# Two-layer interaction network: difference of x made on GpSimd from its own buffers, first stage of layer 2 in pieces, a third buffer for sums of products

## Chip, cores, metric

One core of a Trainium2 chip. The metric is the device time of one execution in microseconds (us). "Span" is the time from the first to the last instruction of the profiled execution, some 1.7 us less. Engines: PE is TensorE (PEld its weight loads), DVE VectorE, ACT ScalarE, POOL GpSimd, SP SyncE, which only issues loads here.

## The reference, cut

```python
# x: 4096 rows, 32 fields, 16 values; all float32
def _cin_layer(out, x, W, b, gamma, beta):
    h = jnp.einsum('rne,rfe->rnfe', out, x).reshape(r, -1, e)    # all products of fields
    h = jnp.einsum('rce,oc->roe', h, W) + b[None, :, None]       # 128 outputs
    return _batchnorm(h, gamma, beta)                            # mean and variance over rows and values
h1 = _cin_layer(x, x, W1, ...)                  # layer 1: 32 x 32 products
out, direct1 = (h1[:, :64], h1[:, 64:])
direct2 = _cin_layer(out, x, W2, ...)           # layer 2: 64 x 32 products
return concatenate([direct1, direct2], axis=1).sum(axis=-1)
```

## The kernel before

The columns (row, value) are cut into 128 tiles of 512. Layer 1 takes one tile after another: two loads of 0.5 MB, one product z on VectorE, five matmuls, three ScalarE copies out of PSUM (the memory that TensorE writes its sums to, in banks). Layer 2 goes in 64 chunks of two tiles, with Strassen's scheme: per chunk four stages, each with two factors f (ScalarE, into PSUM), two products z1 and z2 (VectorE, 128x2048), three sums t of these (GpSimd, not in the first stage) and 14 or 16 matmuls into four PSUM banks. Then `combine` puts the banks together, spread over the stages of the next chunk. z2 needs, beside x, differences of x. These are made in layer 1, one for every 16 chunks, and stored to DRAM:

```python
rpool = one.enter_context(tc.tile_pool(name="rpool", bufs=2))
...
def difference(g):
    xs = []
    for j in (2, 0):
        x = rpool.tile([P, 2 * T], FP, tag="r", name="x")          # the buffers of load_rem
        ...
        nc.sync.dma_start(x, bass.AP(xb.tensor, at, [...]))
        xs.append(x)
    nc.vector.tensor_tensor(xs[0], xs[0], xs[1], ALU.subtract)     # VectorE
    nc.scalar.dma_start(diffs[g], xs[0])                           # issued by ScalarE
...
    with tc.issue_after(loads[-1].ins):                            # loop over the tiles t of layer 1
        if t % 16 == 12 and t // 16 < NC // DIFF:
            difference(t // 16)
...
psum = ctx.enter_context(tc.tile_pool(name="psum", bufs=6, ...))   # banks; a chunk of layer 2 takes 4
tpool = ctx.enter_context(tc.tile_pool(name="tpool", bufs=2))      # sums of products
...
def combine(c, sums_):
    x62, x34, x57, x11 = sums_.banks
    act(both[low], x11[high])                                      # ScalarE
    act(both[high], x11[low], bias=b2[low])
    yield
    add(both, both, x11)                                           # VectorE
    yield
    add(e[:, 0], both, x62)
    yield
    ...
for c in range(NC):                                                # layer 2
    f1 = factor(raw[STAGES[0]], STAGES[0], 0)
    for k, i in enumerate(STAGES):
        z1 = multiply(f1, b, "z")
        if k in (1, 2, 3):
            step()                                                 # one step of the chunk before
        f2 = factor(raw[i], i, 1)
        ...
        z2 = multiply(f2, bx, "z2")
        ...
        if k < 3:
            f1 = factor(raw[STAGES[k + 1]], STAGES[k + 1], 0)
        if k == 0:
            step(2)                                                # both copied, both added
        ...
```

A scheduler places the instructions of each engine in an order of its own; `issue_after` adds an edge only to an instruction on the same engine.

## Time and profile before

2178.69 us, median of 3 runs (2177.85 to 2179.77). Three points of the timeline cut the span: "keep" is the small VectorE copy that ends the statistics of layer 1; "last t of chunk 0" is the matmul that waits for the last sum of products in the first chunk of layer 2; then the end.

| before | us |
|---|---|
| keep starts | 533.1 |
| from keep to the matmul on the last t of chunk 0 | 33.9 |
| from there to the end | 1608.2 |
| span | 2175.2 |

The page's lines by slice (40 equal slices, tenths busy) show TensorE near full nearly throughout, and a granted clock (PEclk) of 9 tenths or more in all but the last slice, where TensorE has run out of work. The dips, stretches of 3.4 or 6.8 us at half clock, are too short to show in such coarse slices. The prediction shows finer windows.

```profile
PE   7998899999999999999999999999999999999995
...
PEclk9999999999999999999999999999999999999998
```

### The profile page before, as it was taken

How to read it: one execution, taken by the hardware profiler on the slowest of the kernel's cores; microseconds unless marked ns; L12 is line 12 of the kernel's file. 1: busy time of each engine (PE TensorE's matmuls, PEld its weight loads, DVE VectorE, ACT ScalarE, POOL GpSimd, SP SyncE). 2: the span in 40 equal slices, each digit the busy share in tenths (PEclk: the TensorE clock that was granted, in tenths of full speed). 3: DMA queues.
4: the chain of work that ended last, by engine and by line, in shares of the span. 5: the costliest groups of instructions: out<-in, count | busy, mean ns of one | idle time of the engine just before them, and what ended most of it. 6: DMA issues, size and time to landing. Idle time of an engine off the chain costs nothing.

```text
span 2175.2 us, 23541 instructions
## 1 busy us (share of the span) xinstructions
PE 2104.6 (97%) x8716; PEld 736.2 (34%) x8716; DVE 1909.9 (88%) x1422; ACT 854.4 (39%) x1221; POOL 1355.8 (62%) x582
## 2 busy tenths in 40 slices
PE   7998899999999999999999999999999999999995
PEld 3333343443333333333333333333333333333331
DVE  7876888887899989999988999998999998999995
ACT  3444444454333333433333333333333333333332
POOL 0000000000888888888888788888788888788884
PEclk9999999999999999999999999999999999999998
DMA  9999999997766777666777666777766777766751
GB/s 344 321 313 316 321 353 332 347 354 239 174 165 165 173 171 173 161 165 165 171 171 173 163 164 161 171 172 171 168 163 160 171 171 174 169 157 163 171 129 39
DMA packets 111700, 440.65 MB, mean 203 GB/s; under 512 B 13024, under 2 KB 13024, under 8 KB 102880
## 3 DMA queue, kind: packets, MB, share of 16 engines
q1 hardware_dynamic: 104992, 416.33, 71.3%
q10 hardware_dynamic: 6592, 22.81, 2.9%
q8 instruction: 68, 1.11, 0.2%
q14 instruction: 48, 0.39, 0.1%
HBM read 417.07 MB, written 22.02 MB: 202 GB/s over the span
## 4 chain that ended last, share of the span: by engine, by line
PE 42%; POOL 27%; DVE 10%; issue 9%; DMA 8%; ACT 2%; SPq 1%; DVEq 0%; POOLq 0%; ACTq 0%
PE x L416 32%; POOL t L432 27%; PE ps L307 9%; DMA b<-in_xb 5%; DVE z L390 4%; DVE z L295 4%; ACT both L383 2%; DMA x<-in_xb 1%; DMA r<-in_xr 1%; DVE stats L97 1%; PE ps L305 1%; DMA a<-in_xa 0%; DVE e L386 0%; DMA h<-kept 0%; SPq L200 0%
## 5 line engine op out<-in xcount | busy, mean ns | idle before, releaser
L416 PE MATMUL x<-z,w_sb 128*64 128x512 f32 x2560 | 1076.3, 594 | 0.0
L416 PE MATMUL x<-z,s_sb 128*64 128x512 f32 x2048 | 954.7, 594 | 4.5 <-DVE z L390 4.5
L432 POOL TENSOR_TENSOR t<-z,z 128x1024 f32<-128x1024 f32 x192 | 456.8, 2379 | 779.7 <-DVE z L390 779.7
L432 POOL TENSOR_TENSOR t<-z,t 128x1024 f32<-128x1024 f32 x384 | 903.1, 2374 | 15.1
L416 PE MATMUL x<-t,s_sb 128*64 128x512 f32 x1536 | 698.4, 594 | 0.0
L383 ACT ACTIVATE f<-a,keep 128x512 f32<-128x512 f32 x512 | 398.3, 778 | 637.9 <-DVE z L390 635.1
L390 DVE TENSOR_TENSOR z<-f,b 128x2048 f32<-128x2048 f32 x256 | 582.5, 2275 | 0.9 <-ACT f L383 0.8
L390 DVE TENSOR_TENSOR z<-f,bx 128x2048 f32<-128x2048 f32 x256 | 582.7, 2276 | 0.0
L416 PEld LDWEIGHTS x<-z,w_sb 128*64 128x64 f32 x2560 | 334.7, 137 | 614.1 <-issue 613.8
L307 PE MATMUL ps<-z,w_sb 128*128 128x512 f32 x1024 | 461.5, 608 | 26.5 <-DVE z L295 26.1
L416 PE MATMUL x<-t,w_sb 128*64 128x512 f32 x768 | 363.4, 596 | 9.4 <-POOL t L432 9.4
L416 PEld LDWEIGHTS x<-z,s_sb 128*64 128x64 f32 x2048 | 281.4, 137 | 228.2 <-issue 222.0
L295 DVE TENSOR_TENSOR z<-a,b 128x2048 f32<-128x2048 f32 x128 | 291.8, 2282 | 46.2 <-DMA b<-in_xb 31.9
L307 PEld LDWEIGHTS ps<-z,w_sb 128*128 128x128 f32 x1024 | 195.0, 194 | 291.5 <-issue 234.3
L416 PE MATMUL x<-z,neg_sb 128*64 128x512 f32 x512 | 230.2, 592 | 0.0
L416 PEld LDWEIGHTS x<-t,s_sb 128*64 128x64 f32 x1536 | 205.3, 137 | 4.0 <-issue 4.0
L263 ACT ACTIVATE e<-ps,bn_sb 128x512 f32<-128x512 f32 x127 | 87.3, 687 | 276.2 <-PE ps L307 210.9
L416 PEld LDWEIGHTS x<-t,w_sb 128*64 128x64 f32 x768 | 100.1, 137 | 241.2 <-issue 172.1
L386 DVE TENSOR_TENSOR both<-both,x 128x512 f32<-128x512 f32 x64 | 44.0, 688 | 142.0 <-ACT both L383 142.0
L383 ACT ACTIVATE u<-e,bn_sb 64x512 f32<-64x512 f32 x64 | 46.2, 722 | 183.3 <-DVE e L386 183.3
L383 ACT ACTIVATE both<-x 64x512 f32<-64x512 f32 x64 | 38.0, 593 | 150.4 <-PE x L416 150.4
L276 ACT ACTIVATE ed<-ps,bn_sb 64x512 f32<-64x512 f32 x128 | 87.4, 683 | 2.7 <-ACT sd L110 0.3
(69 smaller groups left out, 856.3 us busy)
## 6 DMA issues: line engine op xcount, KB each, us to landing
a<-h SPq DMA_DIRECT2D x256, 512.0 KB, 5.0
b<-in_xb SPq DMA_DIRECT2D x128, 512.0 KB, 6.8
a<-in_xa SPq DMA_DIRECT2D x128, 512.0 KB, 5.8
b<-in_xb SPq DMA_DIRECT2D x64, 1024.0 KB, 7.1
bx<-in_xb SPq DMA_DIRECT2D x64, 512.0 KB, 6.1
bx<-x SPq DMA_DIRECT2D x64, 512.0 KB, 7.7
h<-kept ACTq DMA_DIRECT2D x64, 256.0 KB, 5.7
r<-in_xr SPq DMA_DIRECT2D x16, 512.0 KB, 6.7
```

Of the source, the lines that this page charges most:

```text
L97: done = nc.vector.bn_stats(self.stats[:, t % SG, :], h)
L263: nc.scalar.activation(e, ps, AF.Identity, bias=b1)
L276: nc.scalar.activation(ed, ps[KEEP:, :], AF.Identity, bias=b1[KEEP:])
L295: nc.vector.tensor_tensor(z, a.rearrange("p (a t) -> p a t", a=2).unsqueeze(2).to_broadcast([P, 2, 2, T]), b.rearrange("p (b t) -> p b t", ...
L305: nc.tensor.matmul(ps, w1_sb[rows, 4 + s // 4, :], zr[rows, :], start=True, stop=False)
L307: nc.tensor.matmul(pss[t], w1_sb[:, m, :], z[:, m // 2, m % 2, :], start=False, stop=(m == 3))
L383: return queue("act", lambda: nc.scalar.activation(to, source, AF.Identity, **scale_bias))
L386: return dve(lambda: nc.vector.tensor_tensor(to, x, y, ALU.add))
L390: dve(lambda: nc.vector.tensor_tensor(z, a.unsqueeze(1).to_broadcast([P, 4, T]), b, ALU.mult))
L416: queue("pe", lambda: nc.tensor.matmul(self.of[x], w, b, start=start, stop=stop))
L432: queue("pool", lambda: nc.gpsimd.tensor_tensor(to, x, y, op))
```

## The change

Intent: take the differences off VectorE, whose order they interrupt, and give them buffers of their own; spread three of the four over layer 2, where DMA and GpSimd have room; start the first matmuls of layer 2 after a quarter of z1 and z2; keep GpSimd from waiting for a buffer of t. To make room, two pools are halved (`spool`, `rpool`). Core of the diff:

```diff
+    xpool = ctx.enter_context(tc.tile_pool(name="xpool", bufs=1))
...
+    def load_x(g, k):
+        x = xs[k] = xpool.tile([P, 2 * T], FP, tag=f"x{k}", name="x")
+        ...
+    def difference(g):
+        done = nc.gpsimd.tensor_tensor(xs[1], xs[1], xs[0], ALU.subtract)
+        nc.scalar.dma_start(diffs[g], xs[1])
+        return done
+    EARLY = [(12, lambda: load_x(0, 1)), (16, lambda: load_x(0, 0)), (28, lambda: difference(0))]
...
-                if t % 16 == 12 and t // 16 < NC // DIFF:
-                    difference(t // 16)
...
-    tpool = ctx.enter_context(tc.tile_pool(name="tpool", bufs=2))
+    tpool = ctx.enter_context(tc.tile_pool(name="tpool", bufs=TB))      # TB = 3
...
     for c in range(NC):
+        if c % DIFF == 2 and c // DIFF + 1 < NC // DIFF:
+            with tc.issue_after(loads[-1].ins):
+                for k in range(2):
+                    load_x(c // DIFF + 1, k)
+        if c % DIFF == 6 and c // DIFF + 1 < NC // DIFF:
+            queue("pool", lambda: difference(c // DIFF + 1))
...
+            if c == 0 and k == 0:
+                f2 = factor(raw[i], i, 1)
+                for j in range(4):
+                    multiply(z1, f1, b, j, j + 1)
+                    multiply(z2, f2, bx, j, j + 1)
```

## The prediction

> **What bounds the kernel now.** I read the busy windows first, then the list of waits, then the timeline at each wait of TensorE, then the chain of work that ended last. A window line has: stretch in us, busy us (and count) of PE, PEld, DVE, ACT, POOL, then the granted TensorE clock, the DMA share and GB/s.
>
> ```profile
> 60.00:80.00 20.00, 19.05 (x43) 8.05 (x44) 16.18 (x14) 9.18 (x15) 0.00 (x0) 0.83 0.98 365
> ...
> 120.00:140.00 20.00, 15.38 (x38) 6.23 (x37) 15.40 (x13) 7.28 (x12) 0.00 (x0) 0.91 0.92 313
> ...
> 180.00:200.00 20.00, 14.09 (x29) 5.95 (x29) 11.06 (x10) 6.57 (x11) 0.00 (x0) 0.83 0.90 284
> ...
> 260.00:280.00 20.00, 16.11 (x38) 6.84 (x39) 16.91 (x14) 9.69 (x15) 0.00 (x0) 0.83 0.96 346
> ...
> 440.00:460.00 20.00, 20.00 (x56) 8.66 (x53) 18.88 (x17) 9.97 (x17) 0.00 (x0) 1.00 0.96 362
> ...
> 1000.00:1500.00 500.00, 497.02 (x2310) 164.04 (x2308) 457.39 (x321) 185.26 (x258) 421.39 (x180) 1.00 0.71 169
> ```
>
> Layer 1 (to 528.8 us) is bound by TensorE where nothing disturbs it: in the chain, four tiles (32 main and 8 remainder records) take 15.0 us, 3.75 us a tile. It is close to its DMA bound too. Four windows stand out, with few matmuls and a lowered clock: they are the four differences of x. Layer 2 is bound by TensorE at 99.4%; 50.30 us for two chunks in the chain.
>
> ```profile
> DVE x L243 <- DMA x<-in_xb: 32.8, 4, 8.9
> ...
> ACT e L263 <- DVE x L243: 29.3, 4, 8.4
> ...
> PE ps L307 <- DVE z L295: 26.1, 9, 5.9
> ...
> PE x L416 <- POOL t L432: 9.4, 32, 0.9
> ```
>
> The difference stands in VectorE's order before products whose data are there, and VectorE waits 7.5 to 8.9 us for the x load. One of the four:
>
> ```profile
> 124.60 1.23 DVE L243 TENSOR_TENSOR x<-x 128x1024 f32<-128x1024 f32 x1 [8.60 <-DMA x<-in_xb]
> ...
> 125.86 0.36 ACTq L244 DMA_DIRECT2D x<-x  x1
> 126.27 0.69 ACT L263 ACTIVATE e<-ps,bn_sb 128x512 f32<-128x512 f32 x1 [7.09 <-DVE x L243]
> ...
> 128.67 3.82 PE L307 MATMUL ps<-z,w_sb 128*128 128x512 f32 x5 [4.62 <-DVE z L295]
> ```
>
> Note ScalarE here: it holds the store of the difference, stands 7.09 us until the difference exists, and evicts only then. In layer 2 the only wait of TensorE is 0.28 us for a sum of products t, every second chunk. The chain behind it:
>
> ```profile
> 1041.39 0.59 ACT both L383
> ...
> 1042.71 0.04 DVE both L386
> ...
> 1045.51 0.22 DVE e L386
> ...
> 1046.11 2.29 DVE z L390
> ...
> 1048.53 2.38 POOL t L432
> ...
> 1065.23 4.71 POOL t L432 x2
> 1069.94 0.04 issue
> 1069.98 0.64 PE x L416
> ```
>
> When bank x11 of a chunk is done, ScalarE copies it (both), VectorE adds it, makes z1 and z2 of the next chunk's second stage, then GpSimd runs nine t's back to back (3 x 7.13 us), and TensorE needs the last. This loop is 0.45 us longer than TensorE's own work over it (matmul starts 0.88 us apart there, 0.43 elsewhere), so it costs 0.45 us per two chunks, 14 us in all. GpSimd itself waits only for z here, never for a free t.
>
> **What the Trainium skill says.** "TensorE: Matmul & The Clock Gate", Part 1, says that after about 3.4 us of idleness TensorE falls to half clock. The trace agrees: idle stretches of 4.07, 4.62, 5.91 and 4.82 us before layer-1 matmuls, one clock dip each; 4.54 us at the start of layer 2, a dip too. The same page, "Architectural detail", calls ACT and DVE strict FIFO, and "DMA: Bandwidth & Descriptors", section on the anatomy of one DMA, says that a semaphore wait of a DMA is made on the issuing sequencer before dispatch. The trace agrees: the 29.3 us in which ScalarE waited for the difference. "GPSIMD Engine Reference", 4.1, says two-input elementwise work is about twice as slow there as on VectorE: here 2.37 us (t, 128x1024) against 1.23 us (the difference).
>
> **The change, part by part.**
>
> *Differences leave VectorE in layer 1.* Removed: idle TensorE 4.07 + 4.62 + 5.91 + 4.82 = 19.4 us. The dips: 20 x (0.17 + 0.09 + 0.17 + 0.17) = 12.0 us of lost clock. Sum 31.4. Check: at 20 us TensorE had 17 of its 1280 layer-1 records behind it; 1263 x 15/40 = 473.6 us would end layer 1 at 493.6 instead of 528.8, 35.2 us in all; the other 3.8 are small waits for loads. DMA permits it, barely: some 172 MB moved by 520 us, 4.7 MB less now; 167 MB at the 345 GB/s of 240 to 480 us take 485 us, and a last tile needs 8.6 us after its load: about 496. So small waits stay: the 2.4 us of idleness seen at 300 to 420 us where loads of layer 2 come early, about 1 us more for two near-equal bounds, and about 2 us for the difference that remains in layer 1. In the built order its store stands on ScalarE right after tile 11, while its second x load is issued after tile 16's loads. So ScalarE stands about 10 us; TensorE can run tiles 12 to 15 in banks already free and then waits some 2 us. Gain 35.2 - 5.5 = about 29.5 us. I put it between 25 and 32.
>
> *Three differences move to layer 2.* GpSimd has room: 2.4 us in the 3.5 to 4.0 us in which it waits for z between chunks. But the built order puts the store of the difference on ScalarE just ahead of "both" of chunk 5 (21, 37), and the difference itself on GpSimd after all 54 t's of chunks 0 to 5. In the timeline "both" begins at 1041.39 and that GpSimd work ends at 1044.52. So: 1044.52 + 2.38 + 0.44 (difference's end to ScalarE's next work, as at 125.83 to 126.27) = 1047.37; "both" is 6.0 us late, and the whole chain above with it. Through GpSimd that gives 6.0 us at the end. But something comes earlier: with six PSUM buffers and four banks a chunk, the next chunk's third matmul writes the bank that the late chain (e, 1045.51 to 1046.2) must first read; the built order has a wait for VectorE on it. TensorE would stop at about 1047.2 and resume at 1052.2: 5.0 us idle, enough for half clock by this case's record. Add the mean dip, 12.0 / 4 = 3.0 us, less the 0.45 us wait that it covers: 7.6 us. Times 3: 22.8 us lost.
>
> *First stage of layer 2 in pieces.* z1 and z2 become eight 128x512 products. From small VectorE steps here, 0.60 us apart, eight take 4.8 us against 2 x 2.2: 0.4 us more; with factor buffers released later, the second stage begins about 0.75 us later. TensorE begins 3.2 us earlier (after 1.3 us, not 4.5) and escapes the dip. But chunk 0 ends on GpSimd: TensorE waits for its last t at 566.97, and that chain starts at the second stage's z2. So no gain; 0.75 us lost.
>
> *Third t buffer.* GpSimd never waited for a t buffer, so nothing: 0.
>
> Sum: -29.5 + 22.8 + 0.75 = -6. Hence 2178.7 - 6 = about 2172 us.
>
> **The rivals.**
> 1. *The moved differences are free* (as intended: the store does not hold ScalarE). Only layer 1 counts: about 2149. Against it: the layer-1 trace, where ScalarE stood behind just such a store, four times of four. For it: GpSimd's free slot.
> 2. *The third buffer also ends the waits for t*: up to 14 us more, 2135 with the first rival, 2158 with my stalls. Against it: GpSimd's t's stand end to end, and what ends its idleness is always z.
> 3. *Layer 1 turns to its DMA bound, or the remaining difference costs as much as the old ones* (ScalarE stands, VectorE's statistics behind it, loads are asked for late): gain 18 to 22 us, time about 2180. For it: DMA share 0.98 to 1.00 at 300 to 420 us. Against: TensorE loses only 2.4 us there.
> 4. *Stalls without a dip*: 6.0 us each, 18 in all, about 2168.
>
> **Range and chances.** Layer 1 at 25 to 32 and stalls at 15 to 26 us give 2162 to 2181 as the corners; I stretch low for the first rival. Over 2% faster means below 2135, which needs both rivals 1 and 2; over 2% slower, above 2222, has no mechanism behind it. Within 2%: 97%.
>
> **What would show each step.** Right: layer 1 ends near 499; no window from 80 to 490 with a clock under 1.00; in chunks 6, 22 and 38 (about 690, 1090, 1500 us) ScalarE's "both" waits for GpSimd's x some 6 us, TensorE waits once about 5 us for VectorE, clock dips follow; a chunk with the difference takes about 32 us in place of 25; one 0.28 us wait for t per two chunks stays. Wrong: those three chunks look like their neighbours (then near 2149), the waits for t vanish (the third buffer worked), or layer 1 still ends after 508.

## The result, and the profile after

2170.06 us, median of 4 runs (2167.60 to 2172.99), against 2178.52 (2177.85 to 2179.77, 4 runs) for the kernel before: ratio 0.9961, 95% interval 0.9944 to 0.9978, so within 2%.

| | before | after | difference |
|---|---|---|---|
| keep starts | 533.1 | 505.5 | -27.6 |
| from keep to the last t of chunk 0 | 33.9 | 34.7 | +0.9 |
| from there to the end | 1608.2 | 1625.6 | +17.4 |
| span | 2175.2 | 2165.9 | -9.3 |

So the change gains 27.6 us in layer 1 and gives 17.4 us of it back in layer 2. Windows of the changed kernel that answer to those of before (same columns):

```profile
60.00:80.00 20.00, 19.13 (x47) 7.74 (x44) 12.91 (x11) 7.94 (x13) 2.35 (x1) 0.96 0.91 305
...
180.00:200.00 20.00, 20.00 (x59) 8.12 (x58) 17.76 (x15) 10.79 (x17) 0.00 (x0) 1.00 0.94 341
...
1000.00:1500.00 500.00, 491.47 (x2263) 161.54 (x2261) 447.68 (x315) 183.36 (x254) 414.29 (x177) 1.00 0.70 166
```

From 180 to 200 us TensorE now does 59 matmul records (a matmul leaves two) at full clock instead of 29 at 0.83. But in 500 us of layer 2 it does 2263 instead of 2310. The list of waits points to the cause (who <- for whom: us in all, times, longest):

```profile
ACT both L387 <- POOL x L160: 25.0, 3, 8.4
...
PE x L426 <- POOL t L442: 18.6, 40, 1.2
...
ACT e L269 <- POOL x L160: 11.9, 1, 11.9
...
PE x L426 <- DVE both L390: 5.8, 3, 1.9
```

L160 is the difference on GpSimd. ScalarE waits for it four times, because it holds the store: three times ahead of "both" in layer 2, once ahead of an eviction in layer 1. TensorE waits for "both" three times, a wait that the kernel before does not have. One of the three in the chain of work (start, us, what):

```profile
1071.70 2.31 POOL t L442
1074.01 2.33 POOL x L160
...
1076.35 0.33 ACTq L161
...
1076.72 0.59 ACT both L387
...
1078.04 0.04 DVE both L390
...
1100.55 4.70 POOL t L442 x2
1105.24 0.04 issue
1105.29 1.07 PE x L426 x3
```

Last t of a chunk, difference, issue of the store, and only then "both", z, the nine t's of the next chunk and TensorE. Before the change, "both" began 3.1 us before that last t ended.

### The profile page after: what moved, and what is told of

Read it like the earlier page. It is cut to its first block, busy times and chain, and to the rows that moved or that the text cites. A ratio compares the mean times of both kernels' runs of the same rounds, so it can differ in the third digit from the quotient of the medians.

```text
span 2165.9 us, 23579 instructions
## 1 busy us (share of the span) xinstructions
PE 2104.0 (97%) x8716; PEld 735.6 (34%) x8716; DVE 1908.1 (88%) x1424; ACT 854.6 (39%) x1221; POOL 1364.8 (63%) x586
## 4 chain that ended last, share of the span: by engine, by line
PE 48%; POOL 27%; issue 9%; DVE 8%; DMA 5%; ACT 2%; SPq 0%; ACTq 0%; DVEq 0%; POOLq 0%
PE x L426 34%; POOL t L442 27%; PE ps L313 13%; DVE z L398 4%; DMA b<-in_xb 3%; DVE z L301 2%; ACT both L387 2%; PE ps L311 1%; DMA a<-in_xa 1%; DVE e L390 1%; POOL x L160 0%; DMA x<-in_xb 0%; DMA r<-in_xr 0%; DVE stats L99 0%; SPq L217 0%
## 5 line engine op out<-in xcount | busy, mean ns | idle before, releaser
L398 DVE TENSOR_TENSOR z<-f,b 128x2048 f32<-128x2048 f32 (+1 forms) x259 | 583.0, 2251 | 1.2 <-ACT f L387 1.2
L398 DVE TENSOR_TENSOR z<-f,bx 128x2048 f32<-128x2048 f32 (+1 forms) x259 | 583.1, 2251 | 0.0
L313 PE MATMUL ps<-z,w_sb 128*128 128x512 f32 x1024 | 452.9, 600 | 4.6 <-DVE z L301 4.2
L99 DVE BATCH_NORM_STATS2 stats<-e 128x6 f32<-128x512 f32 x127 | 87.0, 685 | 9.6 <-ACT e L269 9.6
```

The costliest lines, as they stand in the source:

```text
L99: done = nc.vector.bn_stats(self.stats[:, t % SG, :], h)
L313: nc.tensor.matmul(pss[t], w1_sb[:, m, :], z[:, m // 2, m % 2, :], start=False, stop=(m == 3))
L398: lambda: nc.vector.tensor_tensor(z[:, first:end], a.unsqueeze(1).to_broadcast([P, n, T]), b[:, first:end], ALU.mult)
```

## The experiments

Ten kernels ran, all with correct results. Total times scatter by some 8 us from run to run in several of them (by 12 in e10). In the profiled runs it is layer 1 that differs: keep starts anywhere from 502 to 506 us in kernels whose layer 1 is the same. So besides the times I compare the parts of the span, which repeat in layer 2 to within 0.5 us.

| kernel | keep | keep to last t of chunk 0 | from there to the end | median us (fast runs) | ratio to before, 95% |
|---|---|---|---|---|---|
| before | 533.1 | 33.9 | 1608.2 | 2178.5 | |
| changed | 505.5 | 34.7 | 1625.6 | 2170.1 | 0.9961 (0.9944 to 0.9978) |
| e1_store_later | | | | 2146.2 | 0.9857 (0.984 to 0.9875) |
| e2_two_buffers | 505.9 | 34.7 | 1608.0 | 2149.6 | 0.9866 (0.9852 to 0.988) |
| e3_whole_stage | 502.6 | 33.9 | 1608.0 | 2148.6 | 0.9866 (0.9852 to 0.988) |
| e4_twice | 502.1 | 34.7 | 1632.6 | 2174.3 | 0.9983 (0.9969 to 0.9997) |
| e5_chain | 502.6 | 34.7 | 1592.0 | 2131.4 | 0.978 (0.9765 to 0.9795) |
| e6_direct | 505.2 | 32.3 | 1608.0 | 2146.3 | 0.9842 (0.9828 to 0.9856) |
| e7_store_l1 | 499.3 | 1644.1 from keep to the end | | 2146.3 | 0.9849 (0.9834 to 0.9864) |
| e8_all_in_one | 505.1 | 34.7 | 1608.4 | 2151.2 | 0.9867 (0.9853 to 0.9882) |
| e9_all | 502.9 | 1623.8 from keep to the end | | 2127.3 | 0.9765 (0.9751 to 0.9778) |
| e10_before_chain | 534.7 | 33.9 | 1592.0 | 2163.4 | 0.9932 (0.9915 to 0.9949) |

**e1_store_later: does the store's place on ScalarE cost the 17 us?**

```diff
     def difference(g):
         done = nc.gpsimd.tensor_tensor(xs[1], xs[1], xs[0], ALU.subtract)
-        nc.scalar.dma_start(diffs[g], xs[1])
+        if g == 0:
+            store(g)
         return done
+    def store(g):
+        return nc.scalar.dma_start(diffs[g], xs[1])
 ...
+        if c % DIFF == 7 and c // DIFF + 1 < NC // DIFF:
+            with tc.issue_after(lasts["act"].ins):
+                store(c // DIFF + 1)
```

> The changed kernel, but ScalarE's three stores of the layer-2 differences stand one chunk later in its order, where GpSimd has long made the difference. Theory (the store holds ScalarE, so the chain both, z, t starts late): the three waits of ScalarE for x (8.3 us each) and TensorE's waits of 1.9 us for both go, layer 2 gets back 17 us (5.8 us for each of three): about 2152. Rival (the difference costs by occupying GpSimd, or the layer-2 loads of x cost): the time stays near 2168 to 2170, with GpSimd's t's late in those chunks.

Fast runs: 2143.7, 2146.2 and 2151.9 us. The profiled execution fell in a slow state (span 2223.8, clock 0.945), so its parts are not used; e2 and e3, which have the same edit, show 1608.0 us after chunk 0, the figure of before. The difference on GpSimd and its loads in layer 2 are therefore free; the store's place was the whole cost after chunk 0. The medians fall by more, 20 to 24 us (2170.1 against 2146.2 to 2149.6 in e1 to e3); the profiled execution of the changed kernel is its fastest, and what the other 3 to 6 us are stays open.

**e2_two_buffers: is the third t buffer worth anything?** `TB = 3` becomes `TB = 2` on top of e1.

> As e1_store_later, with two t buffers instead of three. Theory (GpSimd never waits for a free t): within 1 us of e1_store_later, the same 0.28 us waits for t every second chunk. Rival (the third buffer keeps waits away that would now be there): 5 us or more slower, with GpSimd waiting for PE before some t's.

1608.0 us after chunk 0 with two buffers, 1608.0 with three (e3). The rare waits of TensorE for t stay in both, and in both GpSimd's t's wait for z alone, never for TensorE to free a t (e2, then e3):

```profile
POOL t L446 <- DVE z L402: 675.6, 65, 443.4
```

```profile
POOL t L446 <- DVE z L402: 672.8, 65, 440.4
```

Worth nothing here.

**e3_whole_stage: are the pieces of the first stage worth anything?** On top of e1, `if c == 0 and k == 0:` becomes `if False:`.

> As e1_store_later, with the first stage of layer 2 whole, as before the change. Theory (chunk 0 ends on GpSimd's chain, which the pieces delay): TensorE is idle 4.5 us again before its first layer-2 matmul and the clock dips, yet the time is 0.5 to 1 us shorter than e1_store_later. Rival (TensorE's earlier start and the missing dip count): 3 to 6 us longer.

The first matmul of layer 2, e2 (pieces) and then e3 (whole):

```profile
508.40 1.11 PE L430 MATMUL x<-z,s_sb 128*64 128x512 f32 x1 [1.45 <-DVE z L402]
```

```profile
508.19 1.11 PE L430 MATMUL x<-z,s_sb 128*64 128x512 f32 x1 [4.54 <-DVE z L402]
```

TensorE is idle 3.1 us less with the pieces, and yet the way from keep to the last t of chunk 0 is 0.87 us longer (34.74 against 33.88). e2 and e3 differ in the t buffers too, but these do not matter for it: the changed kernel, with pieces and three buffers, also takes 34.7, and the kernel before, whole and with two, 33.9. The total times (2149.6 and 2148.6) cannot show so little; the parts of the span do. The early start is thrown away because the chunk ends on GpSimd, which e6 tests.

**e4_twice: doubling the suspected wait.** The changed kernel, with a second subtraction of the same size ahead of the one that counts:

```diff
     def difference(g):
+        if g > 0:
+            nc.gpsimd.tensor_tensor(d1[:, : 2 * T], xs[1], xs[0], ALU.subtract)
         done = nc.gpsimd.tensor_tensor(xs[1], xs[1], xs[0], ALU.subtract)
```

> The changed kernel with GpSimd making each of the three layer-2 differences twice before the store (the first into d1, which is no longer needed). Theory: ScalarE stands 2.4 us longer each time, TensorE's wait for both grows from 1.9 to about 4.3 us, and each stall costs 2.4 us more: 7 us slower than the changed kernel, near 2177; if 4.3 us of idleness bring clock dips, most of a dip hides behind GpSimd's chain, so at most 3 us more. Rival (GpSimd has slack of 3.5 us a chunk and the store does not matter): unchanged, near 2170.

After chunk 0: 1632.6 against 1625.6 us, 7.0 more. In the profiled runs the spans differ by only 3.5 us, since layer 1 happened to be 3.5 us shorter in e4's. The medians are 4 us apart (2174.3 and 2170.1), too near, given their scatter, to show the 7.0 by themselves. The waits:

```profile
ACT both L389 <- POOL x L162: 32.2, 3, 10.8
...
PE x L428 <- DVE both L392: 13.0, 3, 4.4
```

Each is 2.4 us longer, the length of one subtraction, and each of the three stalls now has a clock dip (3.4, 6.8 and 3.4 us at half clock); the changed kernel had one, in its third. The dips add nothing to the 7.0: they hide behind GpSimd's chain, as expected.

**e5_chain: what makes the rare waits for t?** On top of e1, the addition of "both" goes behind z1 of the second stage:

```diff
-                if k in (1, 2, 3):
-                    step()
+                if k in (1, 2, 3):
+                    step(2 if k == 1 else 1)
 ...
             if k == 0:
-                step(2)
+                step()
```

> As e1_store_later, with VectorE's add of both moved behind the product z1 of the second stage, so that z1 fills the 2 us in which VectorE waits for ScalarE. Theory (the loop x11, both, z1, e, z2, nine t's, TensorE is 0.45 us longer than TensorE's own work, and this makes all waits for t): the loop is some 2 us shorter, the 0.28 us waits for t go, and the time from the last t of chunk 0 to the end falls by 32 x 0.45 = 14 us, from 1608 to about 1594; the whole near 2134. Rival (GpSimd's own rate or a t buffer makes the waits): nothing changes.

1592.0 us after chunk 0 instead of 1608.0. Windows of layer 2, from 560 to 2100 us, e3 and then e5:

```profile
560.00:2100.00 1540.00, 1533.33 (x7104) 504.74 (x7102) 1410.11 (x988) 574.57 (x797) 1298.62 (x554) 1.00 0.72 167
```

```profile
560.00:2100.00 1540.00, 1540.00 (x7180) 515.49 (x7178) 1426.27 (x995) 578.37 (x802) 1314.78 (x561) 1.00 0.71 167
```

In this window TensorE is busy without a gap. Nothing was removed: VectorE does the same work in an order that fills its 2 us of waiting for ScalarE.

**e6_direct: is chunk 0 on the chain through VectorE and GpSimd?** On top of e1, `nc.vector.tensor_copy(direct[...], ss1[high, 0:3:2])` becomes `nc.scalar.activation(direct[...], ss1[high, 0:3:2], AF.Identity)`.

> As e1_store_later, with the two copies of 2.1 us each that VectorE makes in chunk 0 (direct) made by ScalarE. Theory (chunk 0 ends on the chain VectorE, GpSimd, TensorE, and GpSimd waits 2.4 us there for a z that the copies delay): from keep to the last t of chunk 0 it takes 2.4 us less, 32.3 in place of 34.7; all else stays. Rival (TensorE's work bounds chunk 0): 34.7 stays.

32.3 us instead of 34.7, and 1608.0 as ever after it. Two copies of 64x2 elements were worth 2.4 us, because GpSimd waited for the z behind them. The wait, as the changed kernel has it (first) and gone in e6 (second):

```profile
526.01 2.36 POOL L442 TENSOR_TENSOR t<-z,z 128x1024 f32<-128x1024 f32 x1 [2.43 <-DVE z L398]
```

```profile
523.27 2.38 POOL L446 TENSOR_TENSOR t<-z,z 128x1024 f32<-128x1024 f32 x1
```

In the kernel before, the copies took VectorE 1.85 and 2.30 us, each ending when GpSimd's running t ended (547.96 against 547.93, 550.26 against 550.24); ScalarE takes 0.20 us for one. That the copy waits for GpSimd's instruction is only argued from these ends.

**e7_store_l1: the store left in layer 1.** On top of e1, `store(0)` is called in tile 36 behind that tile's eviction (`issue_after` that ScalarE instruction), not with the difference.

> As e1_store_later, with the store of the one difference that is left in layer 1 placed after tile 36 on ScalarE instead of after tile 11. Theory: ScalarE's wait for x (11.9 us) goes, with the idle TensorE and the clock dip near 80 to 95 us that follow it; keep is ready 2 to 4 us earlier, near 501 to 502 at the latest, and the runs scatter less. Rival (loads bound layer 1): keep stays at 502 to 506.

Keep starts at 499.3, and the wait of ScalarE for x is gone. Windows of the changed kernel (80 to 100 us; its 60 to 80 us stand above, with 47 records), of e7, and of e5, in which the store is still in its old place:

```profile
80.00:100.00 20.00, 20.00 (x50) 8.41 (x50) 18.99 (x18) 10.16 (x17) 0.00 (x0) 0.95 0.99 341
```

```profile
60.00:80.00 20.00, 20.00 (x58) 8.44 (x58) 18.66 (x15) 9.82 (x16) 2.35 (x1) 1.00 0.93 337
80.00:100.00 20.00, 20.00 (x53) 8.57 (x52) 18.20 (x15) 11.24 (x18) 0.00 (x0) 1.00 0.99 349
```

```profile
60.00:80.00 20.00, 19.15 (x53) 7.88 (x54) 13.97 (x13) 8.90 (x14) 2.34 (x1) 1.00 0.96 326
80.00:100.00 20.00, 20.00 (x53) 8.48 (x52) 20.00 (x18) 10.47 (x17) 0.00 (x0) 1.00 1.00 364
```

So the store starves TensorE: from 60 to 80 us it does 58 records in e7 and in e9, where the store is moved too, and 45 to 53 in the six fast profiles with the store in its old place. The clock dip is gone in e7, but this alone does not show that the store makes it: e4 and e5 (52 and 53 records) have no dip there either; the changed kernel, e2, e3 and e6 (45 to 50 records) have one. The gain in keep is one execution's: e9, with the same layer 1, has 502.9. From keep to the end e7 takes 1644.1 us, 1.3 more than e2, with a dip of 3.4 us in chunk 0. The median equals e1's; the runs spread over 5.4 us (2144.9 to 2150.2), against 6.5 to 8.2 in e1 to e3, too few runs to call it less. So in total time the gain of a few us is not shown, and where the rest of the scatter comes from stays open.

**e8_all_in_one: was the move to layer 2 needed?** The changed kernel with all four differences in layer 1, one each 24 tiles, loads 8 and 4 tiles ahead of the subtraction, stores placed late on ScalarE, none in layer 2:

```diff
+    DIFFS = []
+    for g_ in range(NC // DIFF):
+        DIFFS += [
+            (24 * g_ + 4, lambda g=g_: load_x(g, 1)),
+            (24 * g_ + 8, lambda g=g_: load_x(g, 0)),
+            (24 * g_ + 12, lambda g=g_: difference(g)),
+        ]
 ...
+            if t % 24 == 18 and t < 96:
+                with tc.issue_after(acts[-1].ins):
+                    store(t // 24)
```

> The changed kernel with all four differences made on GpSimd in layer 1 (one each 24 tiles, loads 8 tiles ahead, the store placed late on ScalarE), none in layer 2. Theory (it was VectorE's place and the shared buffers that cost, not the transfers): layer 1 ends within 4 us of the changed kernel, 4.7 MB more at 345 GB/s being 13.6 us of transfers of which most fit beside TensorE's work; layer 2 without stalls takes 1608 us after chunk 0: about 2150. Rival (layer 1 is at its DMA bound, so that the move to layer 2 was needed): layer 1 ends 10 us or more later, about 2160.

Keep starts at 505.1, as in the changed kernel; 2151.2 us in all. The 4.7 MB fit, if barely: TensorE loses 3.8 us once, at 323 us, where loads of layer 2 come on top. So it was not the transfers that cost 27.6 us in the kernel before. e8 takes away the place on VectorE, the shared buffers and the store right behind the difference all at once; what each of them cost, no run tells. Nor does a run undo the halved pools.

The Trainium skill ("GPSIMD Engine Reference", section 8) says that GpSimd contends with VectorE instructions that have two inputs in SBUF (the on-chip memory). The products of layer 1 have two, and the trace of e8 agrees. A difference that begins at 128.07 us, while a product runs to 130.00, takes 4.16 us instead of 2.35; the next product begins at 131.14, while that difference runs to 132.23, and takes 3.23 instead of 2.29. The difference at 218.35 does the same (3.88, and 3.22 for the product). Each is longer by about the time for which the other was still running. In layer 2, where one input of z lies in PSUM, the three differences of the changed kernel took 2.34 to 2.36 us.

**e9_all and e10_before_chain.** e9 is e5, e6, e7 and e3 together. e10 is the kernel before with nothing but the edit of e5.

> All that helped, together: stores of the layer-2 differences one chunk later, the layer-1 store after tile 36, both added behind z1, direct copied by ScalarE, first stage of layer 2 whole. If the parts are independent: keep ready at 499 to 502, chunk 0 some 31.5 us (34.7 less 2.4 less 0.9), 1592 us after it: 2125 of span, about 2126 in all, 0.976 of before. Rival (the parts share a bound, as when TensorE's own work bounds chunk 0 once its chain is shorter): chunk 0 stays above 32, time near 2129.

> The kernel before, with nothing but both added behind z1. Theory (the 0.45 us loop makes all waits for t, with two t buffers as well as three): 16 us less after chunk 0, 1592 in place of 1608, about 2163. Rival (it needs the third t buffer): less than 5 us gained, and GpSimd waits for PE before t.

e9: 2127.3 us (2125.8 to 2128.4), ratio 0.9765, faster than both kernels and the best of this study. The waits of TensorE for t are gone, the whole stage costs its idle 4.5 us and a dip of 6.8 us, and from 508.5 us on nothing but TensorE stands in the chain. The times are those of the theory: 31.4 us to the matmul on the last t, which no longer waits, 1592.4 after it, 2127.3 in all where 2126 was expected and 2129 by the rival. Of the rival its mechanism is right: with the chain of chunk 0 short, TensorE's own work bounds it, and the pieces, useless in the changed kernel, would now, by estimate, meet the other bound at about the same time (from keep, 32.3 us in e6, whose chunk 0 still ends on GpSimd, plus 1592.0 is 1624.3, against 1623.8 measured in e9).

e10: 2163.4 us (2157.6 to 2169.3), 1592.0 after chunk 0: 15 us of 2178 for moving one addition, in the kernel before, with two t buffers.

## Why the prediction was right, point by point

- **Layer 1** was put at a gain of 29.5 us (25 to 32); measured 27.6. Removing the four idle stretches and the dips behind them is the gain, as said. Of the 35.2 us at most, 5.5 were held back for small waits; 7.6 were lost. The sentence that no window from 80 us on would show a lower clock was wrong: ScalarE stood 11.9 us (10 predicted) behind the remaining store, TensorE starved near 75 us, and a dip of 3.4 us followed. e7 and e9 show that this store starves TensorE; that a dip follows each time is not so (e4, e5). (485 us and 8.6 us make 493.6, not 496, so the floor set by the loads was no higher than TensorE's own.)
- **Layer 2, the store ahead of "both"** was the point that decided most: predicted from the order of the built kernel, and shown by e1 with e2 and e3 (undone: 17 us back) and e4 (doubled: 7.0 us more, of 7.2).
- **The size of a stall** is the mis-sized term: 7.6 us predicted, 17.4 / 3 = 5.8 measured. The delay through GpSimd alone, 6.0 (its sum gives 1047.34, not 1047.37), was right, and stalls without a dip were the prediction's own rival 4 (18 us in all). Too large was what I put ahead of it: TensorE idle for 5.0 us, waiting for the bank that e reads last, and so a dip each time. In the trace the wait is for "both" (over at 1078.73 us, where e begins at 1080.85), and is 1.94 us; only one of three stalls has a dip. I had counted the six PSUM buffers round in turn; the release says that the third matmul writes the bank that the addition of "both" reads.
- **The pieces of the first stage**: 0.75 us lost predicted, 0.87 measured; e3 takes it back. The dip that they were to escape is absent in the changed kernel but stands in e2 (3.4 us, at 508 us), after an idle stretch of 1.45 us.
- **The third buffer**: 0 predicted, 0 measured (e2). That the waits for t come from a loop 0.45 us too long, at 14 us in all, was a claim about the kernel before; e5 and e10 gain 16 us by shortening that loop.
- The sum, -6, against -9.3 in the profiled runs: the gain in layer 1 was put 1.9 us too high, the loss in layer 2 5.4 us too high, that in chunk 0 0.1 too low. The errors partly cancelled; that the total came so close, 2172 against 2170, is luck in part.

## What to carry to other kernels

In these runs a store's issue waited on the engine that issues it, for the data, and everything behind it in that engine's order waited too (ScalarE up to 8.4 us a time in layer 2): when work moves to another engine, look where the scheduler has put the issue that depends on it, and pin it behind work that is late enough. Before shortening a wait, follow its chain round to itself; a loop that is half a microsecond longer than the bottleneck's own work costs that much at every turn, and moving one small instruction into an idle slot can end it where another buffer does nothing. An earlier start gains nothing where the stretch ends on another engine.

## What the Trainium skill lacked or had wrong

- "TensorE: Matmul & The Clock Gate", Part 1, gives about 3.4 us of idleness for the fall to half clock, and says of short pauses between groups of matmuls that they make the clock swing too, without a length. After the first 20 us, waits of 3.8 us and more had a dip in every profile here. But one of the changed kernel's three waits of 1.94 us had one too (at 1487 us), and so did the starved stretch near 75 us, where TensorE did 47 matmul records in 20 us (58 in e7) and stood still for only 0.87 us.
- The same page knows half and full clock, 13/16 with three busy cores of a die, and traces stuck at a quarter. One execution of e1, on one core, ran from 17 us to the end of its matmuls at 0.949 (span 2223.8 us in place of some 2145). What caused it is open.
